# Two transformer layers on one core: other operands for the start-up products, the first loads in another order, and one copy ahead of four exponentials

## The chip, the cores and the metric

The kernel runs on one core of a Trainium2 chip. The metric is the time of one execution on the device in microseconds (us); lower is better. Before the change it is 731.13 us, the median of three runs (730.96, 731.13 and 732.91). One more execution was recorded by the hardware profiler; it took 732.8 us, and from its first instruction to its last it spans 731.0 us.

## The reference, cut to what matters

Input are 4 sequences of 256 tokens with 256 features. Four blocks follow each other, each ending in a residual sum and a layer norm. The first is the one that the change touches: attention with 16 heads, each with 128 plain and 64 rotary features.

```python
q, k, v = x @ Wq.T, x @ Wk.T, x @ Wv.T
q_rope, k_rope = rope(q[..., 2048:]), rope(k[..., 2048:])
scores = q_nope @ k_nope.T / sqrt(128) + q_rope @ k_rope.T / sqrt(64)
x = layernorm(x + (softmax(scores) @ v) @ Wo.T)
x = layernorm(x + ffn0(x))      # silu(x W1) * (x W3), Hadamard transform, W2
x = layernorm(x + mlstm(x))     # gated linear attention, with its own small MLP
x = layernorm(x + ffn1(x))      # int8 weights with scales
```

All arithmetic is float32 (the last block splits its values into two rounded parts). The output is the last `x`.

## The kernel before, in words

The whole program is written out as straight-line code for the five engines: TensorE (PE) multiplies, ScalarE (ACT) evicts products from PSUM and computes exponentials, VectorE (DVE) takes maxima and normalizes, GpSimd (POOL) rotates, SyncE (SP) issues most of the loads. A planner puts each engine's instructions in order, in the main in the order of the text, and adds the semaphores. `tc.issue_after(x)` tells it that what follows inside is queued behind `x`, where both are on the same engine.

**Tiling of the attention.** The heads are taken in eight pairs (`p`) and the four sequences in two halves (`n`), so that there are 16 steps `h = 2p + n`. The input stands transposed in SBUF in `xT` (128 partitions, 2 chunks of 128 features, 1024 tokens); half `n` is columns `n*512` to `n*512+511`. The weights of a pair are one tile `w` of 128 x 2 x 1024: columns 0:256 give q's plain part of two heads, 256:384 q's rotary part, 384:640 k's plain part, 640:768 k's rotary part, 768:1024 the values. The middle index is the chunk of 128 features over which a product is summed, so each product needs both chunks of `w` and of `xT`. POOL copies the two rotary parts into `w_rot` in another column order (L106).

**Units.** `projections(h)` (L151) returns eight units of work: two rotary products (L167), q plain twice (in step 0 both heads in one unit, `nope_q2`, L180, which goes through chunk 0 for both heads and then through chunk 1), k plain twice (L196), values twice (L200). Each is a product into one PSUM bank with the tag "mm", of which there are two, and an eviction: ACT for q, k and the rotary parts, DVE for the values.

**Order at the start.** Lines 383 to 388: the units of step 0 in the order q, k, k, rotary q, rotary k, values, values; then the first four of step 1 (rotary q, rotary k, q, q), which read the second half of `xT`; then `block(0)` (L338).

**A block** computes the scores of step `h` (L220) for both sequences of the half (`ps[0]` and `ps[1]`), and for each the maxima (L251, DVE), the exponentials (L260, ACT), the normalization (L268, L270, DVE) and a block transpose (L278, DVE); DMAs on SP bring the blocks to their places (L285) for the next step. Among these it calls the remaining units of the step after, one at a time by `unit()`. In `block(0)` the units left are k for head 0, k for head 1, values, values. The exponentials of `ps[1]` stand under `tc.issue_after(copied.ins)` (L370), where `copied` is the result of the second `unit()` after the first two; in block 0 that is the eviction of the second values product, which is DVE's, while the exponentials are ACT's.

**Loads at the start.** ACT's queue issues `xT`: chunk 0 of the first half, chunk 1 of the first half (L118), then the whole second half (L120). SP's queue issues `w` of pair 0 in four pieces (L97), the rotary tables (four small transfers, L90), the values' columns of `w` (L99), the other constants (L100), `w_o` (L114), the residual input `acc` (L128), pair 1's `w` (L102) and `w_o`, and the three weights of the next block (L136). A transfer waits on SP until the one issued eight earlier, over both queues, has landed, because eight semaphores are used in turn.

**Start-up products.** Before any input is there, DVE fills a tile `idle` with zeros (L78) and PE multiplies it by itself four times (L81), into a bank that nothing reads. A float32 matmul of the text is recorded as two passes.

Of the kernel before, what the change touches and what calls it, by code (L numbers as in the profile page):

```python
# [9 lines left out]
F32 = mybir.dt.float32  # L10
# [6 lines left out]
P = 128  # L17
# [3 lines left out]
KC = D // P  # L21
# [4 lines left out]
HALF = NT // 2  # L26
# [12 lines left out]
def tile_two_layers(ctx: ExitStack, tc: tile.TileContext, a: dict, out: bass.AP):  # L39
    nc = tc.nc  # L40

    const = ctx.enter_context(tc.tile_pool(name="const", bufs=1))
    small = ctx.enter_context(tc.tile_pool(name="small", bufs=3))
    psum = ctx.enter_context(tc.tile_pool(name="psum", bufs=2, space=bass.MemoryType.PSUM))

    def bank(tag):
        return psum.tile([P, 512], F32, tag=tag, name=f"ps_{tag}")
# [26 lines left out]
    xT = attn.tile([P, KC, NT], F32, tag="xT", name="xT", bufs=1)  # L74


    idle = small.tile([P, 384], F32, tag="idle", name="idle", bufs=1)
    nc.vector.memset(idle, 0.0)  # L78
    ps = bank("pt")
    for _ in range(4):  # L80
        nc.tensor.matmul(ps[:, 0:256], lhsT=idle[:, 0:P], rhs=idle[:, P:], start=True, stop=True)  # L81

    cst = const.tile([P, 1024], F32, tag="cst", name="cst")

    def load_tables():
        for h in range(2):
            for x in range(2):
                rows = slice(h * DR + x, (h + 1) * DR, 2)
                src = a["cst"][h * DR + x * 32 : h * DR + (x + 1) * 32, 0:512]
                nc.sync.dma_start(cst[rows, 0:512], src)  # L90

    def load_pair(p):

        w = attn.tile([P, KC, 1024], F32, tag="w", name="w_qkv", bufs=2)
        if p == 0:
            for lo, hi in ((0, 256), (384, 640), (256, 384), (640, 768)):
                nc.sync.dma_start(w[:, :, lo:hi], a["w_qkv"][p][:, :, lo:hi])  # L97
            load_tables()
            nc.sync.dma_start(w[:, :, 768:], a["w_qkv"][p][:, :, 768:])  # L99
            nc.sync.dma_start(cst[:, 512:1024], a["cst"][:, 640:1152])  # L100
        else:
            nc.sync.dma_start(w, a["w_qkv"][p])  # L102
        wr = attn.tile([P, KC, 2, P], F32, tag="wr", name="w_rot")
        for i in range(KC):
            for k in range(2):
                nc.gpsimd.tensor_copy(  # L106
                    wr[:, i, k, :].rearrange("p (h f x) -> p h f x", h=2, x=2),
                    w[:, i, 256 + 384 * k : 384 + 384 * k].rearrange("p (h x f) -> p h f x", h=2, x=2),
                )
        return w, wr  # L110

    def load_output(p):
        wo = attn.tile([P, 2, D], F32, tag="wo", name="w_o")
        nc.sync.dma_start(wo, a["w_o"][p])  # L114
        return wo

    for i in range(KC):
        nc.scalar.dma_start(xT[:, i, 0:HALF], a["xT"][:, i, 0:HALF])  # L118
    for n in range(1, 2):
        nc.scalar.dma_start(xT[:, :, n * HALF : (n + 1) * HALF], a["xT"][:, :, n * HALF : (n + 1) * HALF])  # L120
    weights, w_os = {0: load_pair(0)}, {0: load_output(0)}
    cos, sin = cst[:, 0:256], cst[:, 256:512]
    had = cst[:, 512:640]
    mask = cst[:, 640:768]
# [2 lines left out]
    for n in range(2):  # L127
        nc.sync.dma_start(acc[n], a["x"][:, n * NJH : (n + 1) * NJH, :])  # L128
    weights[1], w_os[1] = load_pair(1), load_output(1)

    def ff_weight(name, engine=nc.sync, dtype=F32):
# [88 lines left out]
    def scores(t, batches):  # L220

        qn, kn, qr, kr, _ = t
        ps = {bb: [bank(("sc", "pt")[bb]) for _ in range(2)] for bb in batches}
        queries = lambda bb, qt: slice(bb * S + qt * P, bb * S + (qt + 1) * P)
        keys = lambda bb: slice(bb * S, (bb + 1) * S)
        for bb in batches:
            for e in range(2):  # L230
                for qt in range(2):
                    nc.tensor.matmul(  # L232
                        ps[bb][e][:, qt * S : (qt + 1) * S],
                        lhsT=qn[:, e, queries(bb, qt)], rhs=kn[:, e, keys(bb)],
                        start=(qt == 0), stop=False, skip_group_check=True,
                    )
        for bb in batches:
            for qt in range(2):
                for e in range(2):
                    rows = slice(e * DR, (e + 1) * DR)  # L240
                    nc.tensor.matmul(  # L241
                        ps[bb][e][:, qt * S : (qt + 1) * S],
                        lhsT=qr[rows, queries(bb, qt)], rhs=kr[rows, keys(bb)],
                        start=False, stop=(qt == 1), skip_group_check=True,
                    )
        return ps


    def maxima(ps):
        nmax = small.tile([P, 2], F32, tag="nmax", name="nmax", bufs=5)  # L250
        nc.vector.tensor_reduce(  # L251
            nmax, ps.rearrange("p (t k) -> p t k", t=2), AX.X, ALU.max, negate=True
        )
        return nmax
# [11 lines left out]
    def normalized(pr, rsum):  # L266
        rinv = small.tile([P, 2], F32, tag="rinv", name="rinv")
        nc.vector.reciprocal(rinv, rsum)  # L268
        for qt in range(2):
            nc.vector.tensor_scalar(  # L270
                pr[:, qt, :], pr[:, qt, :], rinv[:, qt : qt + 1], None, ALU.mult
            )
        return pr
# [3 lines left out]
    def block_transposed(pr, e, cross):  # L277
        return nc.vector.transpose(cross[:, :, e], pr.rearrange("p t (x i) -> p x t i", i=32))  # L278
# [15 lines left out]
    def crossing():  # L294
        return attn.tile([P, 2, XB, 2, 2, 32], F32, tag="cross", name="cross")
# [14 lines left out]
    def weighted(t, bb, e, probs, po):  # L310
        mm_k(
            po[:, e * S : (e + 1) * S],
            lambda i: t[4][:, 2 * bb + i, e * P : (e + 1) * P],
            probs,
            2,
        )
# [21 lines left out]
    def block(h, t, probs, prev, units):  # L338


        u = iter(units)
        unit = lambda: next(u, nothing)()
        ps = scores(t, (0, 1))
        crossed = crossing()

        def finish(bb, e, found):
            return block_transposed(normalized(*found), e, crossed[:, bb])

        def values_of(bb, between):
            if not prev:  # L350
                between()
                return nothing
            po = bank("ot")
            weighted(prev, bb, 0, probs[bb][0], po)
            between()
            weighted(prev, bb, 1, probs[bb][1], po)
            return output_product(h - 1, bb, po)

        top = [maxima(ps[0][e]) for e in range(2)]
        for e in range(2):  # L360
            done = finish(0, e, exponentials(ps[0][e], top[e]))
            unit()
        if h == 1:
            unit()
            unit()
        first = values_of(0, unit)
        copied = unit()
        with tc.issue_after(done.ins):
            top = [maxima(ps[1][e]) for e in range(2)]
        with tc.issue_after(copied.ins):  # L370
            found = [exponentials(ps[1][e], top[e]) for e in range(2)]
        first()
        finish(1, 0, found[0])
        unit()
        finish(1, 1, found[1])
        out = spread(crossed)
        second = values_of(1, unit)
        unit()
        unit()
        second()  # L380
        return out
# [20 lines left out]
    ps = {}  # L402
# [24 lines left out]
    for c in range(NH // 2):  # L427
        ps = bank("sc")
        nc.tensor.matmul(
            ps, lhsT=had, rhs=src[:, 2 * c : 2 * c + 2, :].rearrange("p c d -> p (c d)"),  # L430
            start=True, stop=True,
# [279 lines left out]
    def between(t, bb):  # L711

        ps = bank("m")
        nc.tensor.matmul(
            ps[:, :HV], lhsT=t["ks"][:, bb].rearrange("p h d -> p (h d)"),
            rhs=t["va"][:, 2 * bb].rearrange("p h d -> p (h d)"), start=True, stop=True,
        )
        state = mix.tile([P, HV], F32, tag="state", name="state", bufs=2)
        nc.vector.tensor_tensor(
            state.rearrange("p (h d) -> p h d", h=H1), ps[:, :HV].rearrange("p (h d) -> p h d", h=H1),  # L720
            own.unsqueeze(2).to_broadcast([P, H1, DV]), ALU.mult,
        )
        yield
        po = bank("m")
        second = slice(bb * S + P, (bb + 1) * S)
        nc.tensor.matmul(po[:, :HV], lhsT=t["qT"][:, second], rhs=state, start=True, stop=True)
        part = mix.tile([P, H1, DV], F32, tag="part", name="part", bufs=2)
        scale = t["tok"][:, 1, 2, 32 * bb : 32 * bb + H1]
        nc.vector.tensor_tensor(
            part, po[:, :HV].rearrange("p (h d) -> p h d", h=H1),  # L730
            scale.unsqueeze(2).to_broadcast([P, H1, DV]), ALU.mult,
        )
        t["part", bb] = part
        yield
# [384 lines left out]
```

## Time and profile before

| | |
|---|---|
| median of three runs | 731.13 us |
| profiled execution, its own time | 732.8 us |
| its span | 731.0 us |
| mean granted TensorE clock | 0.997 |
| PE busy | 719.4 us (98%) |
| DVE, ACT, POOL busy | 398.8, 238.8, 175.1 us |
| start-up products on PE | 1.32 to 5.10 us |
| first product on input (L185) | begins at 6.18 us |
| last product ends | 723.46 us |

Times in the views below are microseconds from the start of the span. In a timeline, a line gives start, duration, engine, line of the program, operation, output and inputs by name, shapes and how many instructions were put together; square brackets give the idle time ahead of it and what ended that. SPq and ACTq are the sequencers that issue DMAs. In a table by windows the number after an engine is its busy time in the stretch, and in parentheses its number of instructions.

### The profile page before, as it was taken

The page shows a single profiled execution, that of the slowest core. Times are in us where ns is not written, and L with a number is a line of the kernel's source. Part 1 is how long each engine was busy: PE and PEld are TensorE (multiplying, and loading weights), DVE is VectorE, ACT ScalarE, POOL GpSimd, SP SyncE. Part 2 cuts the span into 40 slices and gives each one's busy share as a digit, 9 for nine tenths or more (in the row PEclk, how much of TensorE's full clock was granted, in tenths as well). Part 3 has the DMA queues.
Part 4 walks back from the last instruction along what each step waited for, and adds up shares of the span by engine and source line. Part 5 has one row for each costly group of instructions (what it writes and reads, how often), then busy time and mean ns, then how long its engine had stood idle before and what let it go on. Part 6 is the DMA issues. An engine that isn't in the chain of part 4 may idle for free.

```text
span 731.0 us, 8563 instructions
## 1 busy us (share of the span) xinstructions
PE 719.4 (98%) x2956; PEld 485.1 (66%) x2956; DVE 398.8 (55%) x1017; ACT 238.8 (33%) x625; POOL 175.1 (24%) x187
## 2 busy tenths in 40 slices
PE   8999999999999999999999999999999999999995
PEld 4667667667767767766766774655776476747885
DVE  0373544545655364364455555373778458754766
ACT  2232422432342242243233332126521452111553
POOL 0812422439440341243044000002300050000210
PEclk9999999999999999999999999999999999999998
DMA  8542042183133223322311313002130020000001
GB/s 247 212 107 56 18 123 56 25 279 61 29 101 58 44 87 59 62 79 48 72 30 30 58 60 66 0 1 64 55 115 1 23 94 1 0 1 0 1 1 57
DMA packets 48107, 45.34 MB, mean 62 GB/s; under 512 B 9504, under 2 KB 42688, under 8 KB 46016
## 3 DMA queue, kind: packets, MB, share of 16 engines
q1 hardware_dynamic: 46928, 40.47, 21.1%
q0 software_dynamic: 432, 3.15, 1.2%
q10 hardware_dynamic: 704, 1.18, 0.5%
q8 instruction: 23, 0.38, 0.2%
q14 instruction: 20, 0.16, 0.1%
HBM read 25.61 MB, written 1.08 MB: 37 GB/s over the span
## 4 chain that ended last, share of the span: by engine, by line
PE 91%; DVE 4%; ACT 2%; DMA 1%; issue 1%; POOL 0%; DVEq 0%; ACTq 0%
PE ps_mm L69 37%; PE ps_d L69 11%; PE ps_ot L69 8%; PE ps_m L69 8%; PE ps_d L561 5%; PE ps_pt L232 4%; PE ps_sc L232 4%; PE ps_d L861 4%; PE ps_sc L241 2%; PE ps_m L561 2%; PE ps_m L778 2%; PE ps_pt L241 2%; PE ps_mm L185 1%; DMA w_qkv<-in_w_qkv 1%; PE ps_m L534 1%; ACT ex L763 1%
## 5 line engine op out<-in xcount | busy, mean ns | idle before, releaser
L69 PE MATMUL ps_mm<-xT,w_qkv 128*128 128x512 f32 x248 | 115.8, 593 | 0.0
L176 POOL TENSOR_TENSOR rope_raw<-rope_raw,cst 128x512 f32<-128x512 f32 x32 | 40.7, 1271 | 231.8 <-DVE rope_swp L173 224.5
L260 ACT ACTIVATE pr<-ps_sc,nmax 128x256 f32<-128x256 f32 x64 | 29.5, 472 | 142.2 <-DVE nmax L251 142.2
L69 PEld LDWEIGHTS ps_mm<-xT,w_qkv 128*128 128x128 f32 x248 | 47.0, 190 | 37.2 <-issue 33.8
L69 PEld LDWEIGHTS ps_ot<-prT,v 128*128 128x128 f32 x240 | 45.6, 190 | 28.8 <-issue 25.4
L69 PE MATMUL ps_ot<-prT,v 128*128 128x256 f32 x240 | 60.8, 379 | 0.0
L69 PE MATMUL ps_mm<-w_o,oT 128*128 128x256 f32 x256 | 60.6, 380 | 0.0
L69 PE MATMUL ps_mm<-xT,w_rot 128*128 128x512 f32 x128 | 59.0, 604 | 0.0
L270 DVE TENSOR_SCALAR pr<-pr,rinv 128x256 f32<-128x256 f32 x128 | 57.8, 485 | 1.8
L69 PE MATMUL ps_mm<-w_qkv,xT 128*128 128x256 f32 x256 | 58.1, 379 | 0.3 <-ACT kn L198 0.3
L69 PE MATMUL ps_d<-fm,w 128*128 128x512 f32 x128 | 56.7, 594 | 0.3 <-ACT fm L538 0.3
L69 PEld LDWEIGHTS ps_mm<-w_o,oT 128*128 128x128 f32 x256 | 48.4, 190 | 12.9 <-issue 6.0
L69 PEld LDWEIGHTS ps_mm<-w_qkv,xT 128*128 128x128 f32 x256 | 48.6, 190 | 8.1 <-issue 1.0
L251 DVE TENSOR_REDUCE nmax<-ps_sc 128x2 f32<-128x512 f32 x32 | 20.6, 687 | 59.1 <-PE ps_sc L241 59.1
L756 POOL TENSOR_TENSOR ex<-cst,wide 128x512 f32<-128x512 f32 x16 | 19.9, 1264 | 131.7 <-DMA wide<-far 71.0
L210 DVE COPY v<-ps_mm 128x512 f32<-128x512 f32 x32 | 22.0, 691 | 50.4 <-PE ps_mm L69 46.8
L268 DVE RECIPROCAL rinv<-rsum 128x2 f32<-128x2 f32 x64 | 9.7, 152 | 64.2 <-ACT pr L260 64.0
L278 DVE STREAM_TRANSPOSE cross<-pr 128x512 f32<-128x512 f32 x60 | 42.7, 711 | 1.5
L69 PEld LDWEIGHTS ps_d<-fm,w 128*128 128x128 f32 x128 | 24.0, 190 | 27.1 <-issue 24.9
L69 PEld LDWEIGHTS ps_mm<-xT,w_rot 128*128 128x128 f32 x128 | 23.2, 189 | 28.1 <-issue 20.4
L177 POOL TENSOR_TENSOR rope_swp<-rope_swp,cst 128x512 f32<-128x512 f32 x32 | 40.8, 1275 | 0.0
L552 ACT ACTIVATE glu_g<-ps_d 128x512 f32<-128x512 f32 x24 | 14.2, 592 | 67.4 <-PE ps_d L69 67.4
(197 smaller groups left out, 1191.2 us busy)
## 6 DMA issues: line engine op xcount, KB each, us to landing
prT<-cross SPq DMA_DIRECT2D x240, 64.0 KB, 2.1
w_qkv<-in_w_qkv SPq DMA_DIRECT2D x7, 1024.0 KB, 5.1
wide<-far SPq DMA_DIRECT2D x8, 512.0 KB, 4.3
w<-in_w SPq DMA_DIRECT2D x3, 1024.0 KB, 12.7
w_o<-in_w_o SPq DMA_DIRECT2D x8, 256.0 KB, 3.1
acc<-in_x SPq DMA_DIRECT2D x2, 512.0 KB
w_gate<-in_w_gate SPq DMA_DIRECT2D x1, 1024.0 KB, 8.5
w_up<-in_w_up SPq DMA_DIRECT2D x1, 1024.0 KB, 10.4
```

What stands on the lines that cost most here:

```text
L69: nc.tensor.matmul(ps, lhsT=lhs(i), rhs=rhs(i), start=(i == 0), stop=(i == n - 1))
L176: nc.gpsimd.tensor_tensor(by_b(raw), by_b(raw), cs, ALU.mult)
L177: nc.gpsimd.tensor_tensor(by_b(swp), by_b(swp), sn, ALU.mult)
L210: return nc.vector.tensor_copy(v[:, 2 * jj : 2 * jj + 2, :], ps.rearrange("p (t d) -> p t d", t=2))
L232: nc.tensor.matmul(ps[bb][e][:, qt * S : (qt + 1) * S], lhsT=qn[:, e, queries(bb, qt)], rhs=kn[:, e, keys(bb)], start=(qt == 0), stop=Fals ...
L241: nc.tensor.matmul(ps[bb][e][:, qt * S : (qt + 1) * S], lhsT=qr[rows, queries(bb, qt)], rhs=kr[rows, keys(bb)], start=False, stop=(qt == 1 ...
L251: nc.vector.tensor_reduce(nmax, ps.rearrange("p (t k) -> p t k", t=2), AX.X, ALU.max, negate=True)
L260: nc.scalar.activation(pr[:, qt, :], ps[:, qt * S : (qt + 1) * S], AF.Exp, bias=nmax[:, qt : qt + 1], accum_out=rsum[:, qt : qt + 1],)
L270: nc.vector.tensor_scalar(pr[:, qt, :], pr[:, qt, :], rinv[:, qt : qt + 1], None, ALU.mult)
L278: return nc.vector.transpose(cross[:, :, e], pr.rearrange("p t (x i) -> p x t i", i=32))
L561: nc.tensor.matmul(po, lhsT=hT[:, i, j * P : (j + 1) * P], rhs=wd[:, i, :], start=(i == 0), stop=(i == NH - 1))
L861: nc.tensor.matmul(ps, lhsT=lhs, rhs=rhs, start=(k == 0), stop=(k == len(terms) - 1))
```

## The change

Four edits, all of which act in the first 45 us:

1. The start-up products read a constant zero that the program's preamble has stored in one column, given as [128, n] by repeating that column. The zero tile and DVE's memset go; there are five products in place of four.
2. The first piece of pair 0's `w` (columns 0:256, both chunks, 256 KB) is loaded in two transfers of 128 KB, chunk 0 and then chunk 1.
3. The second half of `xT` (512 KB) is issued by SP after all of pair 0's loads and ahead of `w_o`, no longer by ACT as its third transfer.
4. In block 0 alone, `copied` is the result of the second `unit()` of the loop, that is ACT's copy of k for head 1, and so the exponentials of `ps[1]` are queued on ACT behind that copy.

```diff
-    idle = small.tile([P, 384], F32, tag="idle", name="idle", bufs=1)
-    nc.vector.memset(idle, 0.0)
+    zeros = lambda n: nc.const_aps.tensor(0.0, [P, n])
     ps = bank("pt")
-    for _ in range(4):
-        nc.tensor.matmul(ps[:, 0:256], lhsT=idle[:, 0:P], rhs=idle[:, P:], start=True, stop=True)
+    for _ in range(5):
+        nc.tensor.matmul(ps[:, 0:256], lhsT=zeros(P), rhs=zeros(256), start=True, stop=True)
...
         if p == 0:
-            for lo, hi in ((0, 256), (384, 640), (256, 384), (640, 768)):
+            for i in range(KC):
+                nc.sync.dma_start(w[:, i, 0:256], a["w_qkv"][p][:, i, 0:256])
+            for lo, hi in ((384, 640), (256, 384), (640, 768)):
                 nc.sync.dma_start(w[:, :, lo:hi], a["w_qkv"][p][:, :, lo:hi])
...
     for i in range(KC):
         nc.scalar.dma_start(xT[:, i, 0:HALF], a["xT"][:, i, 0:HALF])
-    for n in range(1, 2):
-        nc.scalar.dma_start(xT[:, :, n * HALF : (n + 1) * HALF], a["xT"][:, :, n * HALF : (n + 1) * HALF])
-    weights, w_os = {0: load_pair(0)}, {0: load_output(0)}
+    weights = {0: load_pair(0)}
+    nc.sync.dma_start(xT[:, :, HALF:], a["xT"][:, :, HALF:])
+    w_os = {0: load_output(0)}
...
         for e in range(2):
             done = finish(0, e, exponentials(ps[0][e], top[e]))
-            unit()
+            evicted = unit()
...
         copied = unit()
+        if not h:
+            copied = evicted
         with tc.issue_after(done.ins):
             top = [maxima(ps[1][e]) for e in range(2)]
         with tc.issue_after(copied.ins):
             found = [exponentials(ps[1][e], top[e]) for e in range(2)]
```

## The prediction, made before the changed kernel was run

> **What bounds the kernel now.** I read the page first (busy shares), then the stretches of the start, PE's and SP's timelines, PE's waits, and ACT's timeline around the fourth edit. First the page:
>
> ```profile
> span 731.0 us, 8563 instructions
> PE 719.4 (98%) x2956; PEld 485.1 (66%) x2956; DVE 398.8 (55%) x1017; ACT 238.8 (33%) x625; POOL 175.1 (24%) x187
> ```
>
> PE is busy 98% of the span, so time can be had only where PE waits or runs slowly. PE's timeline of the first 13 us, the stretches, and its waits in the first 80 us:
>
> ```profile
> 1.32 3.78 PE L81 MATMUL ps_pt<-idle 128*128 128x256 f32 x8 [1.32 <-DVE idle L78]
> 6.18 5.82 PE L185 MATMUL ps_mm<-xT,w_qkv 128*128 128x512 f32 x8 [1.07 <-DMA w_qkv<-in_w_qkv]
> 11.83 1.55 PE L69 MATMUL ps_mm<-xT,w_qkv 128*128 128x512 f32 x3
> ```
>
> ```profile
> core 0: us, PE busy (x) PEld busy (x) DVE busy (x) ACT busy (x) POOL busy (x), PEclk, DMA share, GB/s
> 5.10:6.20 1.10, 0.03 (x2) 0.05 (x1) 0.00 (x0) 0.00 (x0) 0.00 (x0) 1.00 0.93 257
> 6.20:10.50 4.30, 4.30 (x5) 1.79 (x6) 0.00 (x0) 0.00 (x0) 0.21 (x1) 1.00 1.03 284
> 10.50:12.00 1.50, 1.50 (x5) 0.56 (x4) 0.00 (x0) 0.60 (x1) 0.93 (x4) 1.00 0.96 288
> ```
>
> ```profile
> PE ps_pt L81 <- DVE idle L78: 1.3, 1, 1.3
> PE ps_mm L185 <- DMA w_qkv<-in_w_qkv: 1.1, 1, 1.1
> PE ps_mm L69 <- ACT kn L198: 0.3, 1, 0.3
> ```
>
> Three waits, all in what is edited. Beyond them there is a fourth loss that no wait shows: the first eight 512-wide passes begin at 6.18 and the next product at 11.83, 5.65 us for what takes 8 x 0.43 = 3.44 us later (0.43 is the step from one such pass to the next after 11 us). Single passes begin 0.85 us apart until 10.5 and 0.43 apart from then on; the clock column doesn't show it, but the trace's clock record begins at 10.50. So the slow clock costs 5.65 - 3.44 = 2.21 us in this execution.
>
> ACT's timeline at the fourth edit, then the SP queue:
>
> ```profile
> 36.61 0.59 ACT L198 COPY kn<-ps_mm 128x512 f32<-128x512 f32 x1
> 39.22 0.47 ACT L260 ACTIVATE pr<-ps_pt,nmax 128x256 f32<-128x256 f32 x1 [2.03 <-DVE nmax L251]
> 39.69 0.58 ACT L198 COPY kn<-ps_mm 128x512 f32<-128x512 f32 x1
> 40.15 0.49 ACT L260 ACTIVATE pr<-ps_pt,nmax 128x256 f32<-128x256 f32 x1
> ```
>
> ACT stands idle for 2.03 us with k's second copy behind an exponential that waits for DVE's maximum; PE waits for that copy.
>
> ```profile
> 0.74 2.76 SPq L97 DMA_DIRECT2D w_qkv<-in_w_qkv  x4
> 3.54 3.78 SPq L90 DMA_DIRECT2D cst<-in_cst  x4
> 7.71 0.58 SPq L99 DMA_DIRECT2D w_qkv<-in_w_qkv  x1
> 9.85 0.38 SPq L100 DMA_DIRECT2D cst<-in_cst  x1
> 10.27 0.43 SPq L114 DMA_DIRECT2D w_o<-in_w_o  x1
> 10.85 0.80 SPq L128 DMA_DIRECT2D acc<-in_x  x2
> 11.70 0.43 SPq L102 DMA_DIRECT2D w_qkv<-in_w_qkv  x1
> ```
>
> [...]
>
> **The change part by part.**
>
> *Zero products.* DVE's memset (0.89 to 1.27) goes. The constant is stored by POOL at 0.24 to 0.34 and PE's preamble wait ends at 0.67, so the first pass can begin at about 0.8 (SP and ACT issue at 0.74). Ten passes in place of eight; the step between passes at half clock is 0.427 us, so they run to 0.8 + 4.27 = 5.1 us, against 5.10 now. The fifth product costs nothing as long as the input isn't there before 5.1; without that cover it costs 0.85 us cold, 0.43 warm. No row shows a matmul on a repeated column: I take the same 0.427 (same shape and type); [...]above it is bounded only by the rival below.
>
> *First weights in two.* Today the 256 KB issue at 0.74 and their sixteen parts land between 3.67 and 6.04 us; the first 256 KB of `xT` land from 2.96 to 4.36, its second chunk at 6.85. Half the first weights is half the rows on each DMA engine: the last part at about (2.6 + 6.04) / 2 = 4.3 us, where 2.6 is the first packet. So chunk 0 can start at about 4.5, and the products at max(5.1, 4.5) = 5.1, gaining 6.18 - 5.1 = 1.08 us. The issue of the first piece took 0.70 us, a half should take the 0.38 of a 128-row `xT` transfer: two cost 0.06 us more of SP, hidden. Next late is chunk 1: `xT` chunk 1 lands at 6.85 now, at about 6.6 if the shorter start helps (bounds 6.2 and 6.9). Chunk 0 feeds four passes, 1.72 us warm. With all passes warm the first product can't end before 6.6 + 0.14 + 1.72 = 8.46.
>
> *The clock.* With no gap after 0.8, PE is busy for good. [...] Released at 3.67, the rest of the start-up runs fast and input binds: the product ends at 8.46. Released at 7.08, 5.1 to 7.08 runs at half rate, so it ends at 5.1 + 0.99 + 3.44 = 9.53. [...] I take 8.46: 11.83 - 8.46 = 3.37 us, of which 2.21 is the clock.
>
> *Second half of `xT` on SP.* It follows the constants of L100. These now wait until 9.84, when that half lands; they will wait for a piece of `w` that lands at 7.69, and the half itself for the piece landed at 10.23 (earlier, as 512 KB no longer run beside it). Issued at 10.2 at the latest, it lands between 13.6 (`w_o`, 256 KB, issued at 10.27) and 17.4 (`acc`, 512 KB, issued at 10.85). PE reads it first at 22.25 now, 10.42 after 11.83, so at 8.46 + 10.42 = 18.9: cover 1.5 to 5.3 us. Behind it on SP stand `w_o`, `acc`, pair 1's `w`, its `w_o` and the three later weights, each 0.63 us (its issue on ACT) later. Bytes ahead of pair 1's `w` are the same, only in another order, so it lands near today's 21.2; POOL wants it at 22.5 now, about 19 to 20 then, and may wait 1 to 2 us. Behind that copy are rotary k and step 1's rotation: k is done at 27.4 for scores that need it at 32.66, both 3.4 earlier but for the wait: 5.2 - 2 leaves 3 us. `w_o` and `acc` are wanted after 60 us. ACT loses 0.63 us of issue before 2.3, and nothing waits for ACT until 11.17. Price: 0.
>
> *Exponentials behind the copy.* k's second product ends at about 38.3; the copy then takes 0.59 to 38.9, ahead of the maximum at 39.20. PE's 0.30 wait goes, and the exponentials start no later (cover 0.3 us); they end about 0.5 sooner, since no copy splits them. Gain 0.30.
>
> *Sum* against the profiled execution's own 732.8 us (span 731.0 and 1.8 around): 732.8 - 3.37 - 0.30 = **729.1 us**. The median 731.13 lies 1.7 below the profiled 732.8, the third run 732.91 beside it. [...] I keep 729.1, 0.28% under the median.
>
> **Rivals.** (1) [...]732.8 - (11.83 - 9.53) - 0.30 = 730.2; with a release as long after the first product as now (4.3 us): 5.1 + 2.15 + 3.44 = 10.69, hence 731.4. [...] Against: no gap is left. (2) *The other side: the repeated column is read slowly.* If a pass on it takes 0.85 rather than 0.427, the start-up ends at 0.8 + 8.5 = 9.3, past the input; even warm the product then ends at 12.8: 732.8 + 0.95 - 0.30 = 733.4, slower by 0.3%. It decides from 0.62 us a pass, where the product ends at 10.46 and 731.13 is reached. For it: no row of such an operand. Against: nothing in the trace ties a pass to what it reads. (3) *The second half of `xT` is late*: 1 us for each beyond 18.9; 22.6 would be needed to be slower than 731.13 by 0.3%, and 17.4 is my worst. (4) *The planner orders later work otherwise*: PE's other waits sum to 1.3 us, so it may win 1 at most; lose 1 or more: 730 to 732. (5) *The clock was no loss in most runs and input doesn't come sooner*: 731.13 - 0.30 = 730.8.
>
> **How the numbers follow.** 0.3% (2.2 us) is about what a measurement of this kernel can tell from no change: the borders are 728.9 and 733.3. Forecast 0.56, own range 728.2 to 729.8, since input may come at 6.2 (0.4 less) and base and phase vary by 0.5: of it 0.38 lies below 728.9 and 0.18 above. Rival 1: 0.20 (same). Rival 2: 0.06 (slower). Rival 3: 0.01 (slower). Rival 4: 0.08 (0.02 faster, 0.03 same, 0.03 slower). Rival 5: 0.09 (same). Faster 0.40, same 0.50, slower 0.10. The forecast, rival 1 without its worst end, and rival 5 give the range 728.2 to 730.9.
>
> **What would show it.** Right: ten start-up passes from 0.8 at 0.43 or less, no gap before L185, L185 from about 5, passes 0.43 apart before 7, L185's successor before 9.6; no PE wait for k's copy near 40, k's second copy ahead of the third pair of exponentials; `xT`'s second half landed before 18. Wrong: passes of 0.8 on the constant, a clock release past 9, a PE wait on `xT` near 19 or between two chunks past 7, or new PE waits after 45 us.

## The result, and the profile after

The changed kernel takes 728.99 us, the median of six runs (728.47 to 729.58). Six runs of the kernel before, in the same rounds, have a median of 731.65 (730.46 to 732.91). The ratio is 0.9967, with a 95% interval of 0.9954 to 0.9980: 0.33% faster, by 2.7 us. The profiled execution took 729.58 us, against 732.8 before. The forecast was 729.1.

The busy shares of the changed kernel, then PE's timeline of its first 13 us, with the columns of the views before:

```profile
span 727.8 us, 8568 instructions
PE 717.6 (99%) x2958; PEld 485.2 (67%) x2958; DVE 398.5 (55%) x1016; ACT 238.6 (33%) x625; POOL 174.9 (24%) x187
```

```profile
0.78 3.95 PE L80 MATMUL ps_pt<-const-float32-0.0 128*128 128x256 f32 x10 [0.78 <-PEq L1111]
5.06 3.67 PE L186 MATMUL ps_mm<-xT,w_qkv 128*128 128x512 f32 x8 [0.33 <-DMA w_qkv<-in_w_qkv]
8.56 3.69 PE L69 MATMUL ps_mm<-xT,w_qkv 128*128 128x512 f32 x8
```

The first product on input (L186 now, L185 before) begins at 5.06 in place of 6.18, and its passes are 0.43 us apart (0.50 after the first): the next product begins 3.51 us later, where it took 5.65. The clock's record begins at 3.91 in place of 10.50, still within the start-up, whose ten passes therefore end at 4.72. PE's waits:

```profile
PE ps_pt L80 <- PEq L1111: 0.8, 1, 0.8
PE ps_m L729 <- DVE ex L770: 0.3, 2, 0.2
PE ps_mm L186 <- DMA w_qkv<-in_w_qkv: 0.3, 1, 0.3
PE ps_ot L69 <- ACT prT_pe L308: 0.3, 1, 0.3
PE ps_d L69 <- ACT fm L541: 0.3, 1, 0.3
PE ps_ot L69 <- issue: 0.2, 1, 0.2
```

The wait for k's copy is gone; the last line, a wait at 413.30, is new. ACT's timeline at the fourth edit, and SP's at the start:

```profile
35.06 0.58 ACT L199 COPY kn<-ps_mm 128x512 f32<-128x512 f32 x1 [1.13 <-PE ps_mm L69]
35.95 0.47 ACT L261 ACTIVATE pr<-ps_pt,nmax 128x256 f32<-128x256 f32 x1 [0.31 <-DVE nmax L252]
```

```profile
0.74 0.90 SPq L96 DMA_DIRECT2D w_qkv<-in_w_qkv  x2
1.69 2.00 SPq L98 DMA_DIRECT2D w_qkv<-in_w_qkv  x3
7.21 0.60 SPq L101 DMA_DIRECT2D cst<-in_cst  x1
7.85 0.58 SPq L121 DMA_DIRECT2D xT<-in_xT  x1
8.47 0.60 SPq L115 DMA_DIRECT2D w_o<-in_w_o  x1
```

The copy runs 0.3 us before the maximum is there. The second half of the input is issued at 7.85 and lands at 13.94; PE reads it first at 18.98.

**Where the time went, pass by pass.** PE's order on the input is the same in both kernels, so the start of each of its passes can be set against its counterpart. In the changed kernel a pass starts earlier by 1.12 us at the first, by 3.27 from the sixth on (input and clock), by 3.83 after k's copy (another 0.57), by 3.42 after the attention's last step (0.41 given back at about 413), and by 3.42 at the last. What follows PE's last product takes 7.73 us, before 7.56. That leaves the span's 3.25. These are figures of two executions; what differs from run to run comes up below.

### The profile page after: what moved, and what is told of

Same layout as the page of the kernel before. It is cut to its first block, busy times and chain, and to the rows that moved or that the text cites. A ratio compares the mean times of both kernels' runs of the same rounds, so it can differ in the third digit from the quotient of the medians.

```text
span 727.8 us, 8568 instructions
## 1 busy us (share of the span) xinstructions
PE 717.6 (99%) x2958; PEld 485.2 (67%) x2958; DVE 398.5 (55%) x1016; ACT 238.6 (33%) x625; POOL 174.9 (24%) x187
## 4 chain that ended last, share of the span: by engine, by line
PE 92%; DVE 3%; ACT 2%; DMA 1%; issue 1%; POOL 0%; DVEq 0%; ACTq 0%
PE ps_mm L69 38%; PE ps_d L69 11%; PE ps_ot L69 8%; PE ps_m L69 8%; PE ps_d L564 5%; PE ps_pt L233 4%; PE ps_sc L233 4%; PE ps_d L864 4%; PE ps_sc L242 2%; PE ps_pt L242 2%; PE ps_m L564 2%; PE ps_m L781 2%; PE ps_m L537 1%; ACT ex L766 1%; PE ps_m L750 1%; DMA w_qkv<-in_w_qkv 1%
```

## The experiments

All durations are of one profiled execution each; "next" is the start of the product after the first one on input, "clock" the start of the trace's clock record at full rate. Ratios are against runs of the kernel before in the same rounds. The changed kernel was run in the first rounds alone, so where its median is set beside that of another run, the rounds differ. Between large sets of rounds each of the two groups into which the runs of the kernel before fall (see below) shifts by up to 0.25 us; differences of that size say nothing. The runs stand in the order in which they are told.

| run | median (range), runs | ratio (95%) | first, next | clock |
|---|---|---|---|---|
| before | 731.65 (730.46 to 732.91), 6 | | 6.18, 11.83 | 10.50 |
| changed | 728.99 (728.47 to 729.58), 6 | 0.9967 (0.9954 to 0.9980) | 5.06, 8.56 | 3.91 |
| zeros_only | 731.09 (730.14 to 732.83), 14 | 0.9995 (0.9984 to 1.0005) | 6.09, 11.37 | 9.66 |
| loads_only | 730.08 (729.32 to 730.59), 16 | 0.9974 (0.9965 to 0.9983) | 4.90, 9.14 | 6.51 |
| copy_only | 730.98 (729.65 to 732.52), 22 | 0.9990 (0.9981 to 0.9999) | 5.96, 11.79 | 10.64 |
| six_idle | 731.81 (730.62 to 732.10), 13 | 0.9996 (0.9987 to 1.0006) | 6.09, 9.60 | 4.44 |
| no_zeros | 728.73 (727.90 to 729.67), 6 | 0.9956 (0.9943 to 0.9969) | 4.63, 8.06 | 4.35 |
| half_on_act | 730.69 (730.00 to 731.17), 9 | 0.9977 (0.9967 to 0.9986) | 4.44, 9.96 | 3.58 |
| one_transfer | 730.07 (729.32 to 730.22), 5 | 0.9969 (0.9956 to 0.9981) | 5.72, 9.23 | 3.72 |
| no_startup | 730.52 (729.84 to 731.44), 14 | 0.9982 (0.9974 to 0.9991) | 4.43, 10.01 | 8.58 |
| ten_zero | 731.46 (730.37 to 732.33), 14 | 0.9995 (0.9986 to 1.0004) | 7.27, 10.70 | 4.99 |
| split_input | 729.60 (729.31 to 730.34), 9 | 0.9972 (0.9961 to 0.9983) | 4.33, 8.98 | 5.99 |
| last_spread | 730.49 (729.58 to 731.38), 22 | 0.9980 (0.9973 to 0.9986) | 4.79, 8.22 | 4.38 |
| last_spread_pinned | 729.35 (728.82 to 730.11), 6 | 0.9970 (0.9958 to 0.9982) | 4.54, 7.97 | 3.87 |

The theory: two losses at the start, late input and a clock that a gap keeps at half rate, plus one wait for a copy. Its first rivals: the zero products alone make the gain, or the loads were hidden anyway.

### One edit at a time

**The zero products alone** (the first hunk of the change on the kernel before).

> The kernel before with the first edit alone: five products on the repeated zero column, from 0.78 us. Theory (input and clock are two losses that add up): input still comes at about 6.0, so L185 still begins at about 6.2 and a gap of about 1 us stays; the start-up is 0.5 us longer, so the clock is released ahead of the input in more executions: the product ends at 9.6 where it is, at about 11.8 where it is not; median about 731.0, 0.1% under before. Rival (the start-up products alone make the gain): about 729.3.

Its PE timeline:

```profile
0.78 4.61 PE L80 MATMUL ps_pt<-const-float32-0.0 128*128 128x256 f32 x10 [0.78 <-PEq L1107]
6.09 5.44 PE L184 MATMUL ps_mm<-xT,w_qkv 128*128 128x512 f32 x8 [0.70 <-DMA w_qkv<-in_w_qkv]
```

The gap stays, 0.70 us, and with it the slow passes: the ratio can't be told from 1. The rival falls. The runs of the kernel before in these rounds, 53 in all, form two groups: 25 lie from 730.13 to 731.49 (median 730.8), 28 from 732.01 to 734.21 (732.8), and none between. (In 22 and 38 runs of later rounds they are there again, less cleanly parted.) The moment at which the clock is released would explain them, but this is inferred: the traces of the kernel before, of this run and of copy_only, with releases from 9.66 to 10.64, are all of executions in the upper group, and none in the lower group was traced. This run's split in the same way, 9 about 730.9 and 5 about 732.6, a larger share in the lower group than before's 25 of 53; 14 runs are too few to make anything of that.

**The loads alone** (the second and third edit).

> The kernel before with the second and third edit alone: first weights by chunk, second half of the input on SP. Theory: input is there at about 5.0, so L185 begins at about 5.1, right behind the four old start-up products (1.32 to 5.10), with no gap; [...]the product ends at 8.6 to 9.7: about 729.8, 0.25% under before, most of the whole gain. Rival (the loads were hidden anyway, the zeros did it): 731.3 or more.

```profile
1.32 3.78 PE L81 MATMUL ps_pt<-idle 128*128 128x256 f32 x8 [1.32 <-DVE idle L78]
4.90 4.41 PE L187 MATMUL ps_mm<-xT,w_qkv 128*128 128x512 f32 x8
```

As expected: the product on input follows the old start-up with no gap, all 16 runs lie within 1.3 us, and the upper group is gone. The clock was released at 6.51 here, when PE had not stood still since 1.32; the kernel before stands still from 5.10 to 6.18. The ratio has 0.26% of the 0.33%. The median is 1.1 us over the changed kernel's, and 1.35 over that of no_zeros (below), a kernel that has the copy besides and is otherwise the same. The copy is worth 0.57 in the traces, as the next run shows; what the rest is stays open.

**The copy alone** (the fourth edit).

> The kernel before with the fourth edit alone. Theory: PE's wait of 0.30 us near 40 goes and stays gone: the time from the end of L185 to PE's last product falls by 0.30; median 731.3, too little for the clock to be told apart by times, so the trace decides. Rival: a wait further on takes its place (in the changed kernel one of 0.18 at 413 was new), 0.1 or nothing left.

Its PE timeline after k's second product, sixteen passes in one piece where the kernel before had two pieces of eight with the wait between them:

```profile
38.08 3.62 PE L69 MATMUL ps_mm<-w_qkv,xT 128*128 128x256 f32 x16
```

Against the kernel before, a pass starts 0.05 us earlier ahead of that place and 0.61 after: the edit is worth 0.57 us, the same as in the changed kernel (3.27 to 3.83) and, within 0.01, in all ten traces that have it; in loads_only and zeros_only, which don't, nothing changes at that place. The profile's wait of 0.30 had shown half of it. Passes before the wait are 0.216 us apart and one's recorded end lies 0.38 after its start, so 0.16 of the stop lies under the recorded end of the pass ahead of it; and the pass after the wait was followed by the next at 0.32 in place of 0.216. With the 0.30 these make 0.56. The expectation had 0.30, read from the idle time. The runs fall into two groups again, of eleven each, about 729.85 and 732.11: 0.9 and 0.7 under the two of before, somewhat more than the trace shows. Then 0.25 of the trace's gain is given back at 416, so the rival is partly right too; that place comes up below.

### Is it the gap that keeps the clock low?

**Six start-up products on the old zero tile**, and nothing else.

```diff
-    for _ in range(4):
+    for _ in range(6):
         nc.tensor.matmul(ps[:, 0:256], lhsT=idle[:, 0:P], rhs=idle[:, P:], start=True, stop=True)
```

> The kernel before with six start-up products in place of four and nothing else: the start-up fills the gap ahead of the first input. Theory (the gap keeps the clock at half rate in part of the executions): [...]the start-up ends at 6.2 to 6.4, the product at 9.7 to 10.5; times between 730.5 and 731.5 with a spread of under 1.2 us, where before spreads by 2.4. Rival (the slow passes have another cause, or the gap doesn't matter): as before plus 0.26, 731.9, spread unchanged.

The clock was released at 4.44, and the next product begins at 9.60, 2.2 us sooner. But this trace doesn't test the gap: at 4.44 PE was still in the first eight passes, which the kernel before has too, and with the clock at full rate the start-up ended at 5.70, so that 0.39 us of gap were left. The 13 runs lie from 730.62 to 732.10, seven of them between the two groups of before, and the median is no better. PE's waits in this execution, which took 731.70, show one reason:

```profile
PE ps_mm L69 <- ACT kn L198: 1.4, 1, 1.4
```

PE waits for k's copy by 1.38 us, not 0.30. ACT and DVE have the same order as before, and POOL's differs in one addition:

```profile
33.57 1.69 DVE L270 TENSOR_SCALAR pr<-pr,rinv 128x256 f32<-128x256 f32 x2
33.59 1.26 POOL L178 TENSOR_TENSOR kr<-rope_raw,rope_swp 128x512 f32<-128x512 f32 x1
38.07 0.47 ACT L260 ACTIVATE pr<-ps_pt,nmax 128x256 f32<-128x256 f32 x1 [3.11 <-DVE nmax L251]
38.53 0.58 ACT L198 COPY kn<-ps_mm 128x512 f32<-128x512 f32 x1
```

The first of the two DVE operations takes 1.43 us, otherwise 0.35, and ends at 35.00, when POOL's addition (to 34.85) is over. The trace of the kernel before has the same slowing: the 96 of these DVE operations that overlap no two-tensor operation of POOL take 0.35 us at most, and the 32 that overlap one have a median of 0.82. How the one holds up the other isn't shown, nor which of them has to come first; here DVE's record begins 0.02 us ahead of POOL's. PE's work had moved up by 2.2 us and POOL's rotation had not; the normalization now fell on it. So the maximum, the exponential and the copy behind it are late. The expectation missed this. The copy ahead of the exponentials, the fourth edit, takes away not only 0.57 us but the way by which such a delay reaches PE. half_on_act, told below, has that edit and meets the same collision; the first DVE operation takes 1.25 us in it:

```profile
33.74 1.27 POOL L179 TENSOR_TENSOR kr<-rope_raw,rope_swp 128x512 f32<-128x512 f32 x1
33.91 1.51 DVE L271 TENSOR_SCALAR pr<-pr,rinv 128x256 f32<-128x256 f32 x2
```

PE waits for no copy there.

What speaks for the gap, then, are the traces whose clock was released after 5.10. Two have start-up and input with no gap between them: loads_only (6.51) and split_input (5.99). Three have a gap of 0.70 to 1.07 us: zeros_only (9.66), before (10.50) and copy_only (10.64). With the groups of runs, which loads_only lacks, this makes a consistent account; an execution of the kernel before with an early release would complete it.

**The changed kernel with no start-up products.**

```diff
-    for _ in range(5):
-        nc.tensor.matmul(ps[:, 0:256], lhsT=zeros(P), rhs=zeros(256), start=True, stop=True)
```

> The changed kernel with no start-up products at all; they compute nothing that is read. Theory [...]: L185 begins at 5.06 as before, its passes are 0.85 us apart until 8.5 to 11.9; 1.7 to 3.4 us over the changed kernel: 730.7 to 732.4. Rival (the clock is let go at a fixed moment, whatever PE does; then the start-up is worth nothing): within 0.3 of the changed kernel.

```profile
4.43 5.75 PE L182 MATMUL ps_mm<-xT,w_qkv 128*128 128x512 f32 x8 [4.43 <-DMA xT<-in_xT]
10.01 3.26 PE L69 MATMUL ps_mm<-xT,w_qkv 128*128 128x512 f32 x7
```

1.5 us over the changed kernel, a little under the 1.7 to 3.4 expected, with the clock released 4.15 us after PE's first pass. PE's first pass moved from 0.78 to 4.43, and the release from 3.91 to 8.58: in these traces the slow passes go with when PE begins to work, and a release at a fixed moment is excluded.

**Ten zero products in place of five** (`range(10)` in place of `range(5)`).

> The changed kernel with ten products on the zero column in place of five. Theory (a start-up product is free only until input is there, about 4.9; beyond that PE's time is the kernel's, 1 to 1): with the clock let go at time r, [...]twenty passes from 0.78 end at 4.66 + r/2, that is at 6.5 to 8.3, and L185 begins there: 1.4 to 2.1 us over the changed kernel, 730.4 to 731.1. Rival (the longer start-up pays for itself by a warmer clock): within 0.3 of the changed kernel.

```profile
0.78 6.65 PE L80 MATMUL ps_pt<-const-float32-0.0 128*128 128x256 f32 x20 [0.78 <-PEq L1111]
7.27 3.59 PE L186 MATMUL ps_mm<-xT,w_qkv 128*128 128x512 f32 x8
```

With the clock released at 4.99, the formula gives 7.16; 7.27 was measured. The median is 2.5 us over the changed kernel, more than the 1.4 to 2.1 expected; the trace accounts for 2.14 (10.70 against 8.56). Start-up work past the landing of input was paid in full here.

### Each edit taken out of the changed kernel

**Without the zero products** (the old tile and four products).

> The changed kernel without its first edit: the zero tile and four products from 1.32 are back. Theory (the start-up ends when input comes in either form; starting 0.54 us sooner only lets the clock go 0.54 sooner in some executions): L185 begins at 4.9 to 5.1 without a gap; at most 0.3 us over the changed kernel, about 729.3, ratio to before 0.9965 to 0.998. Rival (the zeros carry the gain): 730.5 or more.

0.26 us under the changed kernel, with ranges that overlap. L187 (L185 before the change) begins at 4.63 right behind the old start-up. No gain of the first edit can be seen once the loads are in: by the time that input has landed (4.29 here, 4.92 in the changed kernel), either start-up is at its end (4.63 and 4.72).

**The second half of the input on ACT's queue again.**

```diff
+    for n in range(1, 2):
+        nc.scalar.dma_start(xT[:, :, n * HALF : (n + 1) * HALF], a["xT"][:, :, n * HALF : (n + 1) * HALF])
     weights = {0: load_pair(0)}
-    nc.sync.dma_start(xT[:, :, HALF:], a["xT"][:, :, HALF:])
```

> The changed kernel without its third edit: the second half of the input is ACT's third transfer again. Theory A (that half took bandwidth from the first pieces; taking it away brought chunk 1 and k's weights about 1.1 us sooner): chunk 1 lands at 6.5 or later and k's weights at 7.5, L185 still begins at about 5.1, and PE waits by 0 to 0.5 between the chunks: 729.0 to 729.6. Theory B (its place doesn't matter, the split of the weights does it all): equal to the changed kernel within 0.3.

```profile
4.44 3.70 PE L186 MATMUL ps_mm<-xT,w_qkv 128*128 128x512 f32 x8
9.96 3.24 PE L69 MATMUL ps_mm<-xT,w_qkv 128*128 128x512 f32 x7 [1.82 <-DMA w_qkv<-in_w_qkv]
```

Both theories miss; A had the kind of loss right, and its place and size wrong. The first product is as early as ever, and PE then waits 1.82 us for k's weights: they land at 9.83, in the changed kernel at 6.56. The half that is wanted at 19 ran beside the piece that is wanted at 8 and took 3.3 us from it. In these traces it does so only together with the second edit: in the kernel before the half ran beside k's weights too, and they landed at 7.69 (7.55 to 8.01 in the four traces with the half on ACT and no split), where one_transfer, with the half on SP and no split, has 7.27. SP issues k's weights at 1.66 here, behind one transfer more, and ACT the half at 1.68; before it was 1.49 and 1.64. That this order decides is not tested. Without the third edit the change loses 1.7 of its 2.7 us.

**The first weights in one transfer.**

> The changed kernel without its second edit: the first 256 KB of weights in one transfer. Theory (the start of L185 is bound by the landing of the first transfer of weights): it lands at 5.6 to 6.0, L185 begins at 5.7 to 6.2 with a gap of 0.7 to 1.4 us after the start-up: 0.6 to 1.2 us over the changed kernel, 729.7 to 730.3, and more where the gap keeps the clock low. Rival (without the second half of the input beside it, one transfer lands by 5.1): as the changed kernel.

```profile
5.72 3.67 PE L184 MATMUL ps_mm<-xT,w_qkv 128*128 128x512 f32 x8 [1.09 <-DMA w_qkv<-in_w_qkv]
```

As expected: the transfer lands at 5.59, L184 begins at 5.72, and the median is 1.1 us over the changed kernel.

### Can the start be made shorter still?

**The first chunk of input in two transfers by tokens**, chunk 0 of the product in two column halves, four zero products.

```diff
-    for i in range(KC):
-        nc.scalar.dma_start(xT[:, i, 0:HALF], a["xT"][:, i, 0:HALF])
+    for i, lo, hi in ((0, 0, S), (0, S, HALF), (1, 0, HALF)):
+        nc.scalar.dma_start(xT[:, i, lo:hi], a["xT"][:, i, lo:hi])
```

> The changed kernel with the first chunk of the input's first half in two transfers by tokens, chunk 0 of the first product taken in two column halves, and four zero products. Theory (L185 is bound by the landing of its first transfers): 128 KB of input and 128 KB of weights land at 3.9 to 4.4, L185 begins at 4.1 to 4.5 and its product ends when chunk 1 (5.6 to 5.9) has gone through, at 7.5 to 7.7: 0.5 to 0.9 us under the changed kernel, 728.1 to 728.5, where the clock is let go early; nothing where it is late. Rival (what counts is the latency of the first transfer, not its size; or smaller transfers delay chunk 1): equal within 0.3.

```profile
4.33 2.72 PE L186 MATMUL ps_mm<-xT,w_qkv 128*128 128x256 f32 x8
7.19 1.96 PE L191 MATMUL ps_mm<-xT,w_qkv 128*128 128x512 f32 x4
```

The first pieces land by 3.66, but chunk 1 of the input lands at 7.06, in the changed kernel at 5.64, and chunk 1 of the product begins at 7.19. The next product begins at 8.98 in place of 8.56, and the median is 0.6 us over the changed kernel's. The rival's second half holds: with the smaller transfers at the head, what comes behind landed 1.42 us later.

### What is given back at 413?

PE's timeline of the changed kernel at the attention's last step; `ps_ot` is the weighted sum that needs the sixteen moves of L286:

```profile
412.00 1.13 PE L432 MATMUL ps_sc<-w2b,cst 128*128 128x512 f32 x2
413.30 3.69 PE L69 MATMUL ps_ot<-prT,v 128*128 128x256 f32 x16 [0.18 <-issue]
```

SP issues these moves one after another, 0.64 us apart, from 399.96; the last lands at 412.85. The ninth is followed only after 1.79 us, and at that moment one packet of 16,384 bytes is on the queue of kind "instruction". In the kernel before the same place took 1.11 us, and the last move landed at 416.01 for a sum that began at 416.80. What is given back goes with this one stop: in no_zeros and one_transfer the ninth move was followed after 1.25 and 1.32 us, and nothing was given back; in the nine traces where it (or the eleventh, in no_startup) was followed after 1.59 to 1.89, the changed kernel's among them, 0.07 to 0.50 us were. So the loss at 413 is in part the execution's and not the change's. **A quarter of the moves on ACT**, which is idle there:

```diff
-                nc.sync.dma_start(
+                engine.dma_start(
...
+        for c in range(QB - split):
+            move(nc.sync, c)
+        later.append(lambda: move(nc.scalar, QB - 1) if split else None)
```

> The changed kernel with 4 of the 16 moves of the last block transpose issued by ACT, which is idle there, in place of SP. Theory (what the changed kernel gives back at 413, 0.2 to 0.4 us, is SP's chain of 16 moves at 0.64 us each, which PE has caught up with): the moves end 2.5 us sooner, the wait at 413 goes, and the time from the end of L185 to PE's last product falls by 0.2 to 0.4 in the trace; in the times it can hardly be seen (728.7). Rival: PE's work is put in another order there and waits elsewhere: no gain or a loss up to 0.5.

```profile
PE ps_ot L69 <- DMA prT<-cross: 1.2, 1, 1.2
```

The rival won: the planner took the sums ahead of a part of the scores, and PE stood still for 1.2 us at 409.4 for the moves; the median is 1.5 us over the changed kernel's, where the rival allowed 0.5. So the sums were **pinned behind the scores**:

```diff
+    for bb in range(2):
         po = bank("ot")
-        for e in range(2):
-            weighted(prev, bb, e, probs[bb][e], po)
+        with tc.issue_after(scored[0].ins):
+            for e in range(2):
+                weighted(prev, bb, e, probs[bb][e], po)
```

> The run before (4 of the last 16 moves on ACT) with the weighted sums of the last block pinned behind its scores, so that PE keeps the order of the changed kernel. Theory (the wait at 413 is the chain of moves on SP): the last move lands by 411 in place of 412.85, PE doesn't wait near 413, and the time from the next product after L185 to PE's last falls from 711.48 to 711.0 or less; median 728.4 to 729.0. Rival (something else is late there, or another wait takes its place): a wait of 0.1 or more near 413 stays, time as the changed kernel or more.

```profile
411.41 3.72 PE L69 MATMUL ps_ot<-prT,v 128*128 128x256 f32 x16
423.71 0.55 PE L548 MATMUL ps_d<-cst,acc 128*128 128x128 f32 x2 [0.41 <-DVE acc L526]
```

The moves end by 409.2 and the sums start at 411.41 with no wait, so the wait at 413 is the chain of moves. But two products of the Hadamard transform now come behind the sums, and two waits further on (near 423 and 433) are 0.1 and 0.2 us longer: from the next product to PE's last it takes 711.59 us, against 711.48, and the median is 0.36 over the changed kernel's. PE's order was not quite kept, so what the moves alone are worth stays open; no version here beats the changed kernel by more than the runs can tell.

## Why the prediction was right, by its own steps

The forecast 729.1 lies 0.1 from the median, the range 728.2 to 730.9 holds all six runs, and 0.28% was forecast where the ratio says 0.33%, just past the border to "faster by over 0.3%", which had 0.40 and lies inside the measured interval. That the median is hit to 0.1 is in part luck. The sum was made for the profiled execution, with its late clock: of it 3.67 us of gain were forecast and 3.22 came, 729.58; and the median of the six runs lies 0.6 under that.

- **Zero products.** Passes at half rate are 0.43 apart on the repeated column as on the old tile, so rival 2 falls (at 0.43 each from 0.78 the changed kernel's ten passes would have ended near 5.1, an estimate; the clock ended them at 4.72). That the fifth costs nothing held; that the edit earns anything beside the loads isn't seen (no_zeros).
- **First weights in two.** L185 at 5.06 was forecast at 5.1, but not for the reason given. The step took the end of the start-up as the bound and chunk 0 as landed at 4.3; the clock ended the start-up at 4.72, and chunk 0's weights landed at 4.92. And chunk 1 of the input, put at 6.6 and taken as what binds, landed at 5.64 and binds nothing. Two errors of about 0.6 and 1.0 us that cancel: 8.46 forecast, 8.56 measured. The first is this execution's: in the seven other traces with these first loads chunk 0 had landed by 4.29 to 4.47, as forecast. The second is the estimate's: there chunk 1 landed at 5.43 to 5.70.
- **The clock.** That it is released sooner where PE has no gap fits the traces as far as they go (see six_idle above), and the size was right: 2.21 us forecast, 2.14 measured (from the first product on input to the next 3.51, before 5.65). Of the two moments worked through, 3.67 and 7.08, which are the author's assumption, the release at 3.91 is near the first. One near the second is seen in loads_only's execution (6.51), which took 730.14; none of the six runs of the changed kernel comes to the 730.2 of rival 1, with its release at 7.08. The median of before that the forecast was set against came from three runs, two low and one high; with 53 the kernel before is split about evenly.
- **Second half of the input.** "Price: 0" was right for what was asked: it landed at 13.94, between 13.6 and 17.4, and was wanted at 18.98. (Rival 3's 22.6 has a slip: 18.9 and the 4.2 us from 729.1 to 733.3 make 23.1; nothing hangs on it.) The step that was missed is the other side: what the half does to others while it stays on ACT once the first weights are split. It was looked for between chunks of the first product, and was behind it, at k's weights, 1.82 us.
- **The copy.** Mechanism right, size half: 0.30 read off as idle, 0.57 measured from start to start. Of it 0.41 is given back at 413 in the profiled execution, by the chain of moves that was off PE's path before; that was part of rival 4, as an effect of the planner. The planner did change POOL's order at the start (the copies of pair 1's weights behind rotary k), and PE's not at all.

## What to carry to other kernels

At a kernel's start, count three things together: when the first operands land, whether PE has a gap before them, and which later transfer shares the DMA engines with the next operand; here more start-up work ahead of late input gave nothing (zeros_only and six_idle, ratios 0.9995 and 0.9996), input brought forward gave the most (loads_only, 0.9974), and leaving one late-needed transfer in its old place lost 1.7 us (half_on_act). Measure what a wait of PE costs by the starts of the same pass in two traces, not by its idle time, which showed 0.30 of 0.57. And ask what stands behind a waiting instruction: a copy that PE needs belongs ahead of an operation that waits for a third engine (0.57 us here).

## What the runs showed of the hardware beyond that

- **The clock's stretch at full rate.** In the trace's clock record it lasted 716.80 us in the kernel before (from 10.50) and 720.21 in the changed kernel (from 3.91); in the 14 traces it is always one of these two, each in seven. How much PE has to work for the clock to be released isn't shown. Of the 53 runs of the kernel before 25 lie in the lower group, and 47 of the 113 in the three larger sets (42%); of zeros_only's 14 runs 9 lie there. What puts an execution into the one or the other isn't shown either.
- **A stall in the issue of DMAs.** In every trace here one of SP's last moves took longer than the 0.60 us of the others, 1.06 to 1.84 us: the ninth of sixteen in all but the run without the start-up (no_startup), where it was the eleventh, and in the runs with moves on ACT the eighth and the ninth of the twelve left. Each time one 16,384-byte packet of kind "instruction" lies within about 0.25 us of its start. The same holds further ahead: in the changed kernel's trace eight moves in all were followed only after more than 1.2 us, and each began within 0.3 us of such a packet. What ties the two together isn't shown.
- **Transfers side by side.** The sixteen parts of one transfer can land far apart: the first weights' from 3.67 to 6.04 us before, and 128 KB of them from 3.73 to 4.92 after. It is the last part that PE waits for: its first product on input begins at 6.18 and 5.06.
